# A gate stage as one stream of shifted pieces, and a basic block whose bands run ahead in hand order

## The chip, the cores and the metric

The kernel runs on one core of a Trainium2 chip. The time is that of one execution on the device, in microseconds. "Before" is the median of three runs; the profile is one further execution, with its own time.

## The reference

The input x is fp32, of shape 2 x 128 x 128 x 128 (images, channels, rows, columns). Four layers follow each other:

```python
x = layer0(x)   # 3x3 convolution, 8-token mamba scan per pixel, group norm, SiLU, + x
x = layer1(x)   # density gate, see below
x = layer2(x)   # as layer0, with other weights
x = layer3(x)   # basic block, see below
```

The density gate, with 8x8 windows and four groups of 32 channels:

```python
g = x as (B * 4 groups * 16 * 16 windows, 32 channels, 64 pixels)
sq = sum(g * g, -1);  gram = g @ g.T
K = exp(-0.5 * max(sq[:, :, None] + sq[:, None, :] - 2 * gram, 0))
density = K.mean(-1)                      # B x 128 x 16 x 16
y = w2 @ relu(w1 @ density + b1) + b2     # 128 -> 32 -> 128 channels
attn = sigmoid(y) + 0.5
return x * upsample_bilinear(attn, 8)     # back to 128 x 128, corners aligned
```

The basic block, with convolution weights replaced by their signs:

```python
out = relu(batchnorm(conv3x3(x, sign(w1))))
out = batchnorm(conv3x3(out, sign(w2)))
return relu(out + x)
```

Both batch norms take their statistics over the whole batch and all pixels, so each convolution ends before its normalisation begins.

## The kernel before

Channels lie on the 128 partitions. The program is a chain of stages: `_mamba` (layer 0), `_gates` (layer 1), `_mamba` (layer 2), `_basic_block` (layer 3). A mamba layer leaves its result y, before group norm, in device memory; the stage behind it loads y and the layer's input, and makes `Silu(scale * y + bias) + input`. In `_mamba` the order on all engines is written by hand, under `tc.manual_schedule`. In `_gates` and `_basic_block` the Tile planner chooses the order on each engine; instructions that stand outside a hand order can be placed around it. Within an engine, and on the queues on which SP and ACT issue DMAs, instructions run in their order, and one that waits holds those behind it.

**`_gates`.** Work goes by bands of 8 rows: 16 per image, 32 in all, 512 KB each. `load` (L629) loads y and x, applies Silu on ACT (L636) and adds on POOL (L638), into `x1`, a tile with one 8x8 window after another. `turn` (L646) transposes the band on PE (L652) into `pt`; DVE copies it (`xt`, L654), ACT squares it (`xq`, L656) and squares the untransposed band (`sq`, L659), which DVE reduces (`nsq`, L661 and L662). `density` (L665) sums norms and the Gram matrices of all windows in one PSUM tile `pg` (L671 and L681), adds the second norm on DVE (L689), clips on POOL (L695) and takes Exp on ACT (L696). `total` (L699) reduces to densities. Only when an image's last band is through does `gain` (L702) compute the gate for all of its 256 windows: two small products, Relu, Sigmoid, plus 0.5 (L707 to L720). Then `apply` (L722) runs over the image's 16 bands: PE spreads the gains with interpolation weights `ct` (L738, products with K=32 that take one or two of the image's window-row segments at a time), DVE multiplies with the band (L747), and ACT's queue stores it (L751). Image 0's applications alternate with image 1's densities; image 1's come at the end. PSUM has two wide buffers `pt` (3 banks each) and `pg` (2 banks).

**`_basic_block`.** Again 32 bands of 8 rows. `combine` (L814) forms four sums and differences of rows (a Winograd transform in the row direction): number 0 and 3 on POOL (L818, L821), 1 and 2 on DVE (L819, L820). `conv` (L824) does 12 products of 512 columns for the eight rows (L828; each is recorded in two parts, so 24 a band), in the order 1, 2, 0, 3; ACT copies product 1 out (L836), DVE forms the rows of Y (L839 to L842) and their statistics (L844). `convolve` (L860) combines band k + 1 ahead of the products of band k:

```python
ahead = combine(band(*bands[k + 1])) if k + 1 < len(bands) else None
conv(u, v, *at, stats)
```

In the first convolution `band` is `first` (L870): load of y and residual with a border of one row, Silu (L876), add on POOL (L877), and a store of the sum to x3 on ACT's DMA queue (L878). In the second it is `second` (L887): two rows copied from the band before (L894), the others by Relu from Y (L900). Bands have two buffers, `comb` two, `xs` three. The last loop (L908 to L913) loads x3 into one of the three `xs`, takes `Y * s2 + x3` on DVE, Relu on ACT, and stores on ACT's queue.

Of the kernel before, what the change touches and what calls it, by code (L numbers as in the profile page):

```python
# [31 lines left out]
P = 128  # L32
# [59 lines left out]
def _place(k):  # L92


    q = k // 2
    return k % 2 + 2 * (q // 4), q % 4


def _upsampling(H):

    _, fy = _bilinear(H)
    ix, fx = _bilinear(P)
    wx = np.zeros((P // WIN, P), np.float32)
    wx[ix, np.arange(P)] = 1.0 - fx
    wx[ix + 1, np.arange(P)] += fx
    segs = _segments(H)
    up = np.zeros((4, 2, P // WIN, 4, max(e - a for _, a, e in segs), P), np.float32)
    for k, a, e in segs:
        n, g = _place(k)
        for h in range(a, e):  # L110
            up[g, 0, :, n, h - a] = (1.0 - fy[h]) * wx
            up[g, 1, :, n, h - a] = fy[h] * wx
    return up.reshape(P, 4, -1)
# [488 lines left out]
def _gates(tc, src, w, con, y, stats, wm, b1, up, dst, H):  # L602

    nc = tc.nc
# [3 lines left out]
    nwin = nh * nw  # L608
    segs = _segments(H)
    with tc.tile_pool(name="dg", bufs=2) as dp, tc.tile_pool(name="dg1", bufs=1) as sp, tc.tile_pool(  # L610
        name="ps_t", bufs=2, space=PSUM
    ) as pst, tc.tile_pool(name="ps_g", bufs=1, space=PSUM) as psg:

        def wide():
            return pst.tile([P, 3 * ROWS, P], F32, tag="pt", name="pt")

        class Small:


            def tile(self, shape, dtype, tag=None, name=None):  # L620
                return wide().rearrange("p a b -> p (a b)")[: shape[0], : shape[1]]

        norm = [_norm(nc, sp, Small(), w, con, stats, b) for b in range(B)]
        ct = sp.tile([P, 4, up.shape[2]], F32, tag="ct", name="ct")

        dens = [sp.tile([P, nh, 2, npair], F32, tag=f"dens{b}", name="dens") for b in range(B)]
        held, live, gains = {}, {}, {}

        def load(b, y0):  # L629

            rows = slice(y0 * WIN, (y0 + 1) * WIN)
            g = dp.tile([P, WIN, P], F32, tag="g", name="g", bufs=4)
            nc.sync.dma_start(out=g, in_=y[b][:, rows, :])
            xr = dp.tile([P, WIN, P], F32, tag="xr", name="xr", bufs=4)
            nc.sync.dma_start(out=xr, in_=src[b][:, rows, :])
            nc.scalar.activation(g, g, AF.Silu, bias=norm[b][1], scale=norm[b][0])  # L636
            x = held[b, y0] = dp.tile([P, nw, WIN, WIN], F32, tag="x1", name="x1", bufs=nh + 5)
            nc.gpsimd.tensor_tensor(by_row(x), by_row(xr, False), by_row(g, False), ALU.add)  # L638
# [6 lines left out]

        def turn(b, y0):  # L646

            x = held[b, y0].rearrange("p x r w -> p (x r w)")

            pt = wide()[:, :npair, :]  # L650
            for k in range(npair):
                nc.tensor.transpose(pt[:, k, :], x[:, k * P : (k + 1) * P], con["ident"])  # L652
            xt = dp.tile([P, npair, P], F32, tag="xt", name="xt")
            nc.vector.tensor_copy(xt, pt)  # L654
            xq = dp.tile([P, npair, P], F32, tag="xq", name="xq")
            nc.scalar.activation(xq, pt, AF.Square)  # L656

            sq = dp.tile([P, nw, WIN * WIN], F32, tag="sq", name="sq", bufs=1)
            nc.scalar.activation(sq.rearrange("p x r -> p (x r)"), x, AF.Square)  # L659
            nsq = dp.tile([P, nw], F32, tag="nsq", name="nsq")  # L660
            nc.vector.tensor_reduce(nsq, sq, AX.X, ALU.add)  # L661
            nc.vector.tensor_scalar_mul(nsq, nsq, -0.5)  # L662
            live[b, y0] = xt, xq, nsq

        def density(b, y0):  # L665
            xt, xq, nsq = live.pop((b, y0))

            pg = psg.tile([P, 2, 512], F32, tag="pg", name="pg")
# [19 lines left out]
            kk = dp.tile([P, 2, npair, CG], F32, tag="kk", name="kk", bufs=3)  # L688
# [6 lines left out]
            nc.gpsimd.tensor_scalar_min(kk, kk, 0.0)  # L695
            nc.scalar.activation(kk, kk, AF.Exp)  # L696
            live[b, y0] = kk

        def total(b, y0):  # L699
            nc.vector.tensor_reduce(dens[b][:, y0], live.pop((b, y0)), AX.X, ALU.add)  # L700

        def gain(b):  # L702

            den = sp.tile([P, nh, npair, 2], F32, tag="den", name="den")
            nc.vector.tensor_scalar_mul(den, dens[b].rearrange("p y a k -> p y k a"), 1.0 / CG)
            p1 = wide().rearrange("p a b -> p (a b)")[:CG, :nwin]
            nc.tensor.matmul(p1, lhsT=wm["w1"], rhs=den.rearrange("p y k a -> p (y k a)"), start=True, stop=True)  # L707
            hid = sp.tile([CG, nwin], F32, tag="hid", name="hid")
            nc.scalar.activation(hid, p1, AF.Relu, bias=b1)
            p2 = wide()[:, :4, :]  # L710
            gt = gains[b] = sp.tile([P, 4, P], F32, tag="gain", name="gain")
            for n in range(4):
                at = (n % 2 + n // 2 * WIN) * nw
                m = min(P, nwin - at) // 32 * 32
                if m <= 0:
                    continue
                nc.tensor.matmul(p2[:m, n, :], lhsT=hid[:, at : at + m], rhs=wm["w2"], start=True, stop=False)
                nc.tensor.matmul(p2[:m, n, :], lhsT=wm["one"][:, :m], rhs=wm["b2"], start=False, stop=True)
                nc.scalar.activation(gt[:m, n, :], p2[:m, n, :], AF.Sigmoid)
                nc.vector.tensor_scalar_add(gt[:m, n, :], gt[:m, n, :], 0.5)  # L720

        def apply(b, y0):  # L722

            r0 = y0 * WIN
            pu = wide()
            o = dp.tile([P, WIN, P], F32, tag="g", name="o", bufs=4)
            x = by_row(held.pop((b, y0)))

            cut = [a for k, a, _ in segs if k % 2 == 0 and r0 < a < r0 + WIN]
            at = 0  # L730
            for first, end in zip([r0, *cut], [*cut, r0 + WIN]):
                for r in range(first, end, ROWS):
                    for k, a, e in segs:
                        lo, hi = max(a, r), min(e, r + ROWS, end)
                        if lo < hi:
                            n, g = _place(k)
                            q = slice(g * 32, (g + 1) * 32)
                            nc.tensor.matmul(  # L738
                                pu[:, at + lo - first : at + hi - first, :],
                                lhsT=gains[b][q, n, :],  # L740
                                rhs=ct[q, n, (lo - a) * P : (hi - a) * P],
                                start=True,
                                stop=True,
                                tile_position=(q.start, 0),
                            )
                rows = slice(first - r0, end - r0)
                nc.vector.tensor_tensor(  # L747
                    by_row(o[:, rows, :], False), by_row(pu[:, at : at + end - first, :], False), x[:, rows], ALU.mult
                )
                at += (end - first + ROWS - 1) // ROWS * ROWS  # L750
            nc.scalar.dma_start(out=dst[b][:, r0 : r0 + WIN, :], in_=o)  # L751

        order = [(b, y0) for b in range(B) for y0 in range(nh)]
        N = len(order)
        ready = []
        for n in range(-4, N + 2):
            if ready:
                apply(*ready.pop(0))
            if n % 2 == 0:
                for i in range(n + 4, min(n + 6, N)):  # L760
                    load(*order[i])
            if n == -4:
                nc.sync.dma_start(out=ct, in_=up)
            if 0 <= n < N:
                turn(*order[n])
            if 1 <= n <= N:
                density(*order[n - 1])
            if n >= 2:
                b, y0 = order[n - 2]
                total(b, y0)  # L770
                if y0 == nh - 1:
                    gain(b)
                    ready += [(b, i) for i in range(nh)]
        for at in ready:
            apply(*at)


def _basic_block(tc, src, y, norm, x3, w1, w2, bn, out, B, H):
# [6 lines left out]
    with tc.tile_pool(name="bb", bufs=1) as cp, tc.tile_pool(name="bband", bufs=2) as bp, tc.tile_pool(  # L785
# [28 lines left out]
        def combine(xb):  # L814

            v = combined()
            d = [xb[:, k : k + BAND - 1 : 2, :] for k in range(4)]
            nc.gpsimd.tensor_tensor(v[:, 0], d[0], d[2], ALU.subtract)  # L818
            nc.vector.tensor_tensor(v[:, 1], d[1], d[2], ALU.add)  # L819
            nc.vector.tensor_tensor(v[:, 2], d[2], d[1], ALU.subtract)  # L820
            nc.gpsimd.tensor_tensor(v[:, 3], d[1], d[3], ALU.subtract)  # L821
            return v
# [173 lines left out]
```

## Time and profile before

| | |
|---|---|
| median of 3 runs | 7862.33 us (7861.02 to 7884.91) |
| profiled execution | 7862.75 us, span 7860.9 us |
| mean granted TensorE clock | 0.923 of full speed |
| PE busy | 6537.9 us (83%) |
| DVE busy | 6831.1 us (87%) |
| ACT busy | 4291.8 us (55%) |
| POOL busy | 5521.1 us (70%) |
| gate stage, first load to next layer's first load | 3328 to 3638 us |
| first convolution's products | 6980 to 7390 us |
| second convolution's products | 7400 to 7733 us |
| last loop | 7742 to 7861 us |

Busy shares over the whole span say little here: nearly 6900 us of it are the two mamba layers. The stages are read by windows of time. In a table by windows each engine has its busy time and in brackets the instructions counted; then come the granted TensorE clock as a share of full speed, the mean busy share of the 16 DMA engines, and GB/s. In a list of waits each line names who waited and for what it waited last, then the total in us, the number of times and the longest. In the timeline a line has start, length, engine, line of the kernel, operation, tiles and shapes, and in square brackets the idle time before it with its releaser. PEld is the weight load beside PE; SPq and ACTq are issues of DMAs.

### The profile page before, as it was taken

The page shows a single profiled execution, that of the slowest core. Times are in us where ns is not written, and L with a number is a line of the kernel's source. Part 1 is how long each engine was busy: PE and PEld are TensorE (multiplying, and loading weights), DVE is VectorE, ACT ScalarE, POOL GpSimd, SP SyncE. Part 2 cuts the span into 40 slices and gives each one's busy share as a digit, 9 for nine tenths or more (in the row PEclk, how much of TensorE's full clock was granted, in tenths as well). Part 3 has the DMA queues.
Part 4 walks back from the last instruction along what each step waited for, and adds up shares of the span by engine and source line. Part 5 has one row for each costly group of instructions (what it writes and reads, how often), then busy time and mean ns, then how long its engine had stood idle before and what let it go on. Part 6 is the DMA issues. An engine that isn't in the chain of part 4 may idle for free. (4 is left out here: it accounts for less than half of the span.)

```text
span 7860.9 us, 86792 instructions
## 1 busy us (share of the span) xinstructions
PE 6537.9 (83%) x29412; PEld 2217.4 (28%) x29412; DVE 6831.1 (87%) x6360; ACT 4291.8 (55%) x4835; POOL 5521.1 (70%) x1810
## 2 busy tenths in 40 slices
PE   7888888888888888777888888888888888878893
PEld 2222222222222222253222222222222222223341
DVE  5999999999999999863999999999999999963454
ACT  5656666666666656482665665666656656621112
POOL 5777887777778777652777778787777777843330
PEclk8999999999999999866999999999999999979996
DMA  7999999999999999854999999999999999955204
GB/s 203 246 243 246 253 249 247 253 250 256 249 248 254 245 249 248 225 179 127 244 249 246 250 250 251 252 251 253 252 239 249 250 250 250 250 157 139 69 0 163
DMA packets 573435, 1765.42 MB, mean 225 GB/s; under 512 B 85536, under 2 KB 239680, under 8 KB 458176
## 3 DMA queue, kind: packets, MB, share of 16 engines
q1 hardware_dynamic: 530496, 1709.54, 84.0%
q10 hardware_dynamic: 42496, 50.34, 1.8%
q8 instruction: 234, 3.83, 0.2%
q14 instruction: 209, 1.71, 0.1%
HBM read 1549.82 MB, written 209.72 MB: 224 GB/s over the span
## 5 line engine op out<-in xcount | busy, mean ns | idle before, releaser
L451 POOL TENSOR_TENSOR h<-ur,bcr 128x2048 f32<-128x2048 f32 x896 | 4060.4, 4539 | 1193.2 <-DMA bcr<-sb 1006.0
L478 DVE TENSOR_TENSOR set<-set,h 128x1024 f32<-128x1024 f32 x1792 | 2193.0, 1224 | 301.6 <-ACT set L469 216.2
L479 DVE TENSOR_TENSOR r<-set,bcr 128x1024 f32<-128x1024 f32 x1792 | 2194.1, 1224 | 61.4
L469 ACT ACTIVATE set<-set 128x1024 f32<-128x1024 f32 x1792 | 1745.6, 1006 | 868.7 <-PE set L460 854.2
L483 DVE TENSOR_TENSOR h<-set,h 128x1024 f32<-128x1024 f32 x1536 | 1864.5, 1214 | 21.3 <-POOL h L451 21.2
L460 PE MATMUL set<-dt,rep 32*128 32x512 f32 x7168 | 1400.2, 674 | 96.8 <-DVE h L483 89.9
L498 PE MATMUL ys<-r,ct 128*32 128x512 f32 x7168 | 1166.1, 632 | 36.4 <-DVE r L479 36.0
L328 PE MATMUL one<-band,conv 128*128 128x512 f32 x2304 | 1085.5, 607 | 24.6 <-DMA band<-in_x_dram 12.2
L828 PE MATMUL m<-comb,u 128*128 128x512 f32 x1536 | 689.1, 610 | 88.5 <-DVE Y L842 53.2
L406 PE MATMUL one<-xc,keep 128*64 128x512 f32 x1024 | 324.6, 717 | 471.4 <-ACT xc L363 361.5
L460 PEld LDWEIGHTS set<-dt,rep 32*128 32x128 f32 x7168 | 405.2, 193 | 992.7 <-issue 466.2
L328 PEld LDWEIGHTS one<-band,conv 128*128 128x128 f32 x2304 | 408.2, 190 | 674.4 <-issue 599.2
L489 PE MATMUL ys<-t,ct 128*128 128x512 f32 x512 | 326.4, 724 | 252.4 <-DVE v L511 250.9
L357 ACT ACTIVATE xc<-one,keep 128x512 f32<-128x512 f32 x256 | 176.1, 688 | 519.5 <-PE one L355 514.7
L498 PEld LDWEIGHTS ys<-r,ct 128*32 128x32 f32 x7168 | 181.2, 111 | 928.5 <-issue 760.7
L828 PEld LDWEIGHTS m<-comb,u 128*128 128x128 f32 x1536 | 296.6, 195 | 480.3 <-issue 457.3
L426 PE MATMUL one<-prod,ct 128*128 128x512 f32 x512 | 290.3, 650 | 123.1 <-POOL prod L418 88.8
L380 POOL TENSOR_TENSOR u<-dt,xc 128x1024 f32<-128x1024 f32 x128 | 302.8, 2366 | 70.7 <-ACT dt L374 70.6
L355 PE MATMUL one<-y,w_in 128*128 128x512 f32 x512 | 343.5, 759 | 5.8 <-ACT xc L357 3.1
L469 ACT ACT_TABLE_LOAD x252 | 323.3, 1283 | 4.6
L370 PE MATMUL one<-xc,w_dt 128*128 128x512 f32 x512 | 313.5, 696 | 4.1 <-ACT bc L413 4.1
L427 ACT COPY t<-one 128x512 f32<-128x512 f32 x256 | 150.2, 587 | 301.4 <-PE one L426 301.4
(136 smaller groups left out, 5894.0 us busy)
## 6 DMA issues: line engine op xcount, KB each, us to landing
ur<-su SPq DMA_DIRECT2D x896, 896.0 KB, 11.5
bcr<-sb SPq DMA_DIRECT2D x896, 448.0 KB, 11.6
ur<-su SPq DMA_DIRECT2D x896, 128.0 KB, 11.1
su<-u SPq DMA_DIRECT2D x1024, 64.0 KB, 3.5
sb<-bc SPq DMA_DIRECT2D x256, 224.0 KB, 2.8
bcr<-sb SPq DMA_DIRECT2D x896, 64.0 KB, 10.9
y<-o SPq DMA_DIRECT2D x128, 256.0 KB, 9.2
band<-in_x_dram SPq DMA_DIRECT2D x28, 640.0 KB, 10.9
```

The costliest lines, as they stand in the source:

```text
L328: nc.tensor.matmul(py.rearrange("p (r w) -> p r w", r=ROWS), lhsT=w["conv"][:, tap, :], rhs=xb[:, r + kh : r + kh + ROWS, kw : kw + P], st ...
L355: nc.tensor.matmul(p, lhsT=w[("in", "z")[i]][:, g, :], rhs=s["y"], start=True, stop=True)
L406: nc.tensor.matmul(p[g * NQ * DS : (g + 1) * NQ * DS, :], lhsT=w[("xb", "xcm")[i]], rhs=s["xc"][:, g, :], start=True, stop=True,)
L451: nc.gpsimd.tensor_tensor(b, s["ur", t], s["bc", t][:, 0].unsqueeze(1).to_broadcast([P, NJ, NS]), ALU.mult)
L460: nc.tensor.matmul(a[j // 2][:, j % 2, :], lhsT=w["rep"][r, q, :], rhs=s["dt"][r, g, :], start=True, stop=True, tile_position=(r.start, 0),)
L469: nc.scalar.activation(x, x, AF.Exp)
L478: nc.vector.tensor_tensor(pt, pt, s["h", t - 1][:, js, :], ALU.mult)
L479: nc.vector.tensor_tensor(s["r", t][:, js, :], pt, s["bc", t - 1][:, 1].unsqueeze(1).to_broadcast([P, 2, NS]), ALU.mult)
L483: nc.vector.tensor_tensor(s["h", t][:, js, :], pt, s["h", t][:, js, :], ALU.add)
L489: nc.tensor.matmul(s["ys", g], lhsT=con["ident"], rhs=s["t1"][:, g, :], start=True, stop=False)
L498: nc.tensor.matmul(s["ys", g][a : a + NQ * DJ, :], lhsT=red[:, q, :], rhs=r[:, j, :], start=False, stop=(q == NQ - 1), tile_position=(0, a),)
L828: nc.tensor.matmul(m[:, i], lhsT=u[:, i, kw, :], rhs=v[:, i, :, kw : kw + P], start=(kw == 0), stop=(kw == 2),)
```

## The change

The gate stage becomes one stream over all 32 bands. Every band passes through 14 pieces (load and residual ahead of them), each with a lag in steps, in an order written by hand for all five engines:

```diff
+        stages = (
+            (3, density),
+            (6, hide_relu),
+            (8, gate_exp),
+            (1, norms),
+            (2, distance),
+            (0, turn),
+            (4, total),
+            (9, gain),
+            (10, apply),
+            (10, keep),
+            (1, gram),
+            (7, gate),
+            (5, hide),
+            (9, spread),
+        )
+        E = mybir.EngineType
+        with tc.manual_schedule(engines={E.PE, E.Activation, E.DVE, E.Pool, E.SP}):
+            for n in range(-6, N + 11):
+                if n % 2 == 0:
+                    for m in range(max(n + 4, 0), min(n + 6, N)):
+                        load(*order[m])
+                    for m in range(max(n + 2, 0), min(n + 4, N)):
+                        residual(*order[m])
+                for lag, stage in stages:
+                    if stage is gram and 0 <= n + 6 < N and order[n + 6][1] == 0:
+                        b = order[n + 6][0]
+                        norm[b] = _norm(nc, sp, psg, w, con, stats, b)
+                    if 0 <= n - lag < N:
+                        stage(*order[n - lag])
```

The gate is computed for four window rows around a band as soon as these are known, instead of for a whole image; the sigmoid is formed from Exp, an add and a reciprocal; each band is spread by two products with K=64, whose weights are laid out per band (4.19 MB for all bands instead of 2.36 MB):

```diff
+        def gate(b, y0):
+            s = live[b, y0]
+            p = s["pz"] = psg.tile([P, P], F32, tag="two", name="pz")
+            h = hidden[b][:, y0 : y0 + 4, :].rearrange("p y x -> p (y x)")
+            for a in range(0, P, P // 2):
+                nc.tensor.matmul(p[a : a + P // 2, :], lhsT=h, rhs=wm["w2"], start=True, stop=False)
+                nc.tensor.matmul(p[a : a + P // 2, :], lhsT=wm["one"], rhs=wm["b2"], start=False, stop=True)
+
+        def gate_exp(b, y0):
+            s = live[b, y0]
+            s["e"] = dp.tile([P, P], F32, tag="e", name="e")
+            nc.scalar.activation(s["e"], s.pop("pz"), AF.Exp, scale=-1.0)
+
+        def gain(b, y0):
+            e = live[b, y0]["e"]
+            nc.vector.tensor_scalar_add(e, e, 1.0)
+            nc.vector.reciprocal(e, e)
+            nc.vector.tensor_scalar_add(e, e, 0.5)
+
+        def spread(b, y0):
+            s = live[b, y0]
+            pu = s["pu"] = pst.tile([P, 2 * ROWS, P], F32, tag="pt", name="pu")
+            for n in range(2):
+                q = slice(n * P // 2, (n + 1) * P // 2)
+                nc.tensor.matmul(
+                    pu[:, n * ROWS : (n + 1) * ROWS, :].rearrange("p r w -> p (r w)"),
+                    lhsT=s["e"][q, :],
+                    rhs=weights[q, y0, :],
+                    start=True,
+                    stop=True,
+                )
+
+        def keep(b, y0):
+            nc.sync.dma_start(out=dst[b][:, y0 * WIN : (y0 + 1) * WIN, :], in_=live.pop((b, y0))["o"])
```

`hide` and `hide_relu` are the product with w1 and the Relu for one band's 16 windows. `turn`, `norms`, `gram`, `distance`, `density`, `total` and `apply` are the old operations cut into pieces; `apply` is now one multiplication of 128x1024. The two `pt` buffers shrink to two banks each and are shared by the transposes and the spreading. The band stores go to SP's queue. Image 1's normalisation moves from the head of the stage into step 10.

In the basic block three band rooms take the place of two buffers, all four combines go to POOL, and both convolutions get a hand order with loads three bands, making two bands and combining one band ahead:

```diff
-            nc.gpsimd.tensor_tensor(v[:, 0], d[0], d[2], ALU.subtract)
-            nc.vector.tensor_tensor(v[:, 1], d[1], d[2], ALU.add)
-            nc.vector.tensor_tensor(v[:, 2], d[2], d[1], ALU.subtract)
-            nc.gpsimd.tensor_tensor(v[:, 3], d[1], d[3], ALU.subtract)
+            for i, (m, n, op) in enumerate(((0, 2, ALU.subtract), (1, 2, ALU.add), (2, 1, ALU.subtract), (1, 3, ALU.subtract))):
+                nc.gpsimd.tensor_tensor(v[:, i], d[m], d[n], op)
...
+            v = {}
+            E = mybir.EngineType
+            with tc.manual_schedule(engines={E.PE, E.Activation, E.DVE, E.Pool, E.SP}):
+                for k in range(-3, len(bands)):
+                    for ahead, f in ((3, load), (2, make)):
+                        if 0 <= k + ahead < len(bands):
+                            f(k + ahead)
+                    if 0 <= k + 1 < len(bands):
+                        v[k + 1] = combine(k + 1)
+                    if k >= 0:
+                        conv(u, v.pop(k), *bands[k], stats)
...
+        def residual(k):
+            b, r0 = bands[k]
+            xb, lo, hi = span(k)
+            x = xb[:, lo:hi, 1 : P + 1]
             nc.scalar.activation(x, x, AF.Silu, bias=norm[b][1], scale=norm[b][0])
-            nc.gpsimd.tensor_tensor(x, x, xs, ALU.add)
-            nc.scalar.dma_start(out=x3[b][:, r0 : r0 + BAND, :], in_=xb[:, 1 : BAND + 1, 1 : P + 1])
+            nc.gpsimd.tensor_tensor(x, x, rests.pop(k), ALU.add)
+            nc.sync.dma_start(out=x3[b][:, r0 : r0 + BAND, :], in_=xb[:, 1 : BAND + 1, 1 : P + 1])
```

The x3 store moves from ACT's queue to SP's. The rooms' side columns are cleared once instead of for every band. In the last loop the loads of x3 alternate between two `xs` buffers and the two `comb` buffers:

```diff
-        for b, r0 in bands:
-            xr = rest()[:, :BAND, :]
+        for k, (b, r0) in enumerate(bands):
+            if k % 2 == 0:
+                xr = rest()[:, :BAND, :]
             else:
...
+                xr = combined().rearrange("p a b c -> p (a b c)")[:, : BAND * P].rearrange("p (r w) -> p r w", r=BAND)
             nc.sync.dma_start(out=xr, in_=x3[b][:, r0 : r0 + BAND, :])
```

## The prediction

> **What bounds the kernel now.** I read the busy time by stretches first, to see which stages the change touches and what each is limited by.
>
> ```profile
> core 0: us, PE busy (x) PEld busy (x) DVE busy (x) ACT busy (x) POOL busy (x), PEclk, DMA share, GB/s
> 3328.00:3447.00 119.00, 65.50 (x2592) 53.20 (x2592) 67.13 (x84) 110.28 (x105) 72.75 (x37) 0.70 0.64 222
> 3447.00:3460.00 13.00, 11.26 (x162) 6.17 (x162) 7.33 (x14) 9.75 (x13) 2.97 (x2) 0.50 0.00 1
> 3460.00:3570.00 110.00, 96.12 (x2216) 61.26 (x2216) 74.25 (x91) 59.12 (x61) 46.76 (x25) 0.70 0.41 146
> 3570.00:3584.00 14.00, 11.40 (x28) 6.63 (x29) 3.19 (x8) 2.85 (x6) 0.00 (x0) 0.50 0.19 75
> 3584.00:3638.00 54.00, 47.11 (x80) 22.68 (x78) 19.19 (x22) 0.00 (x0) 0.00 (x0) 0.50 0.37 146
> 6980.00:7390.00 410.00, 356.27 (x768) 150.19 (x767) 159.25 (x249) 61.99 (x62) 164.13 (x129) 0.95 0.49 133
> 7400.00:7733.00 333.00, 332.50 (x768) 146.04 (x768) 186.14 (x249) 55.98 (x63) 112.63 (x127) 0.99 0.00 0
> 7742.00:7861.00 119.00, 0.00 (x0) 0.00 (x0) 39.96 (x33) 36.61 (x32) 0.00 (x0) 0.50 0.79 269
> ```
>
> The gate stage (3328 to 3638) takes 310 us in five pieces: image 0's densities (ACT 110 of 119 us busy), its gain, image 1's densities beside image 0's application, the second gain, and an application alone (all PE, at half clock). The two convolutions do the same 768 recorded matmul parts; the second keeps PE busy throughout, the first takes 77 us longer. The last loop uses neither PE nor POOL, and moves 269 GB/s at a DMA share of 0.79. The two mamba layers, ahead of and behind the gate stage, are not touched.
>
> Next, the waits of 6980 to 7390, and one band there in the timeline:
>
> ```profile
> ACT band L876 <- DMA band<-y: 237.8, 30, 16.8
> DVE Y L839 <- ACT m L836: 233.2, 30, 9.0
> POOL band L877 <- ACT band L876: 199.3, 29, 7.5
> ACT m L836 <- POOL band L877: 82.3, 25, 3.8
> PE m L828 <- DVE Y L842: 53.2, 25, 3.9
> ```
>
> ```profile
> 7184.49 0.37 SPq L198 DMA_DIRECT2D band<-y  x1
> ...
> 7189.86 1.45 ACT L876 ACTIVATE band<-band,aff_t,aff_s 128x1280 f32<-128x1280 f32 x1 [8.75 <-DMA band<-y]
> 7191.39 2.68 POOL L877 TENSOR_TENSOR band<-band,xs 128x1280 f32<-128x1280 f32 x1 [6.92 <-ACT band L876]
> ...
> 7194.10 0.42 ACTq L878 DMA_DIRECT2D x<-band  x1
> 7194.62 0.59 ACT L836 COPY m<-m 128x512 f32<-128x512 f32 x1 [3.31 <-PE m L828]
> 7195.24 0.69 DVE L839 TENSOR_TENSOR Y<-m,m 128x512 f32<-128x512 f32 x1 [8.60 <-ACT m L836]
> ```
>
> It is a ring. A band loads (5.4 us), gets Silu (1.45) and the residual (2.7); ACT issues the x3 store, which waits for POOL, and only then evacuates the previous band's product (0.59). DVE's four Y operations (2.4), queued behind that copy, release PE, and the third combine behind them frees a band buffer for the next load. The terms make about 14 us; band loads are issued 12 to 14 us apart, against 10.3 us of products. PE waits for Y although Y is short.
>
> **Conv 1: -77.** The change gives bands three rooms, loads them three ahead, makes them two ahead and combines one ahead; the x3 store leaves ACT's queue for SP's. Evacuation now waits only for PE. PE becomes the bound, as in the second convolution: 410 - 333 = 77 us (24 parts at 0.43 us each, 10.3 us a band). What must stay below 10.3: ACT, 1.45 + 0.59; DVE, 4 x 0.60 + 1.28; POOL, which now does all four combines.
>
> Here the Trainium skill speaks against the change ("GPSIMD Engine Reference", 4.1 Engine selection): an elementwise add belongs on VectorE, GpSimd being about twice as slow with two inputs. The row agrees in size: 1.29 us for a 128x520 combine on POOL alone (L818), 0.69 on DVE (L819). But the rule prices the operation, not the path: POOL needs 4 x 1.29 + 2.69 = 7.85 us a band, 9.7 with the 1.75 us that such a combine takes when it collides with DVE; both are under 10.3. By the rule alone I would add 2 x 0.6 x 64 = 77 us and cancel the gain; by the row I add nothing, as long as the cover of 10.3 us holds.
>
> The order on POOL is copy of the product after PE ends, Silu, add, combine: ready for its first product (combines 0 and 1) 0.6 + 1.45 + 2.7 + 2.6 = 7.4 us after the previous band's end, 2.9 us to spare. SP has 0.37 + 0.32 + 0.42 us of issues a band; the x3 store waits there for POOL's add, with the next loads behind it. They were asked for three bands ahead, and have about 5 us to spare after a 5.6 us landing.
>
> **Starts: +3.** Before the first product POOL does combines 0 and 1 in series (2.6 us) where DVE did number 1 alone (0.7). After the normalisation there is a 0.4 us row copy too: +2.3 us. In conv 1 the weights' preparation hides most of it: +0.7. If the planner places that preparation badly around the hand order, up to 8 more; at best 0.
>
> **Last loop: -18.** Its bands pass through three buffers; now two of xs and two of comb. A round lasts about 11 us (load 4.3, DVE 1.28, ACT 1.15, store 3.6 to 6): 11/3 = 3.7 us a band, as measured (119/32). Four buffers give 11/4 = 2.75, if the queues allow. 269 GB/s at a share of 0.79 means 340 GB/s at 1.0, and a band moves 1.05 MB: 3.1 us. I take 3.2 for 28 bands, with four preloaded: about 101 us, -18. Bounds: -32 at 2.75, -8 at 3.6.
>
> **Gate stage: -41.** Each band now walks through one stream of 32 + 10 steps; the separate gain pauses (27 us) and the lone application (54 us) go. I price one full step by engine.
>
> DVE, start to start: norms 1.40, distance 0.62, copy of the transpose 1.14, total 0.60, apply 1.15, and the gain (three operations of 128x128 in sequence). The adds are 0.23 each (L720). RECIPROCAL appears only as 128x1, at 160 ns against 154 for TENSOR_SCALAR. Low price: 0.23, like the add. High: the Trainium skill ("VectorE: DVE Perf Modes", the walkthrough's hardware budget) says an iterative divide with a repeat count of 8; at 1.05 ns an element (slope from 128x512 to 128x1024) an estimate of 1.2 us. No row excludes either; the 6 ns excess favours the upper, so I take 1.0. Sum 6.4. Small SBUF-only operations are also held up by POOL: L662 has a median of 174 ns but reaches 1473, L720 reaches 2058; mean excesses of 0.2 and 0.35 us, for four operations about 0.8. DVE: 7.2 us (5.6 with a cheap reciprocal and no collision).
>
> ACT: 1.19 Silu, 1.30 table loads (two per two bands), 0.6 Exp, 2.0 Squares, 0.5 for Relu and gate Exp: 5.6. The sigmoid's own table load goes, since Exp serves both. POOL: 2.36 + 1.49 = 3.85. SP: four loads and two stores every second step, 2.2 us of issue in 14; 1.5 MB a step at the 222 GB/s seen here would take 7.1 us, but 408 GB/s were reached at 3335 to 3345, so 3.9.
>
> PE: transposes 1.09 us at full clock (1.97 at half), square sums 0.66 (1.11), Gram 1.5 (1.6), gate 0.43 (0.85), hide 0.1 (0.2), spreading 0.86 (1.7): 4.6 (7.5). The last takes K=64 products in two row halves to run side by side. This line supports that:
>
> ```profile
> 3298.30 1.53 PE L460 MATMUL set<-dt,rep 32*128 32x512 f32 x8
> ```
>
> Eight 512-column parts in 1.53 us, where one after another they would need 3.4. Without overlap, PE is 5.5 to 9.2.
>
> Which clock? The skill's rule ("TensorE: Matmul & The Clock Gate", Part 1) is full rate after one busy window of about 3.4 us. The trace contradicts it here: 3584 to 3638 has PE busy 47 of 54 us and a clock of 0.50 throughout, with K=32 products. By the rule PE needs 4.6 us a step and never decides; by that row 7.5. Mixed with transposes and Gram products the rows show 0.70, so I take about 0.75, 6.0 us, under DVE's 7.2.
>
> Sum: the first Silu 3334 becomes 3336, as the table of upsampling weights ahead of the loads grows from 2.36 to 4.19 MB (the old one landed in 8.8 us). Step 0 takes 8 us (four Silus); steps 1 to 9 follow ACT, 9 x 6.0 = 54; image 1's normalisation in mid-stream 4; 22 steps x 7.2 = 158; ten draining steps 32 (DVE's total, gain and apply, about 3.2 each); the store's landing 4.5. End near 3597 instead of 3638: -41. With the cheap DVE step ACT and DVE, both at 5.6, make about 5.9 with a few waits: 22 x 1.3 = 29 more, -70.
>
> **Total.** The profiled execution took 7862.75 us (span 7860.9, 1.9 around it), 0.4 above the shown median. 7862.75 - 41 - 77 + 3 - 18 = 7729.75, so 7730.
>
> **Rivals.**
> - *PE at half clock becomes the stream's bound* (20%): 7.5 us plus waits for the single Gram buffer, 9.0 a step: 22 x 1.8 = 40 us eat the gate's gain. 7730 + 41 = 7771. For it: the 0.50 row; against: full-array transposes and Gram in every step.
> - *Everything fits better* (12%): 5.9 a step, last loop at 2.75: -70 - 77 + 3 - 32 gives 7687.
> - *The distances are not there in effect* (4%): loads stay queued behind the x3 store on SP, and conv 1 keeps its 12.8 us a band: 7730 + 77 = 7807. Against: three bands' lead.
> - *Slower* (4%): in the stream PE and DVE take turns, since transposes need the copy, Gram the distance's buffer and spreading the gain, all in hand order. The chain: norms 1.4, distance 0.6, square sums and Gram 2.7, gate 0.85, spreading 1.7, transposes 2.0, copy 1.2, total 0.6, gain 1.5, apply 1.15: 13.7 us. With steps 1 to 31 at that and the drain at 6, the stage ends at 3336 + 8 + 4 + 425 + 60 + 4.5 = 3837, 199 later than before: 7862.75 + 199 - 92 = 7970. It decides from 11.1 us a step over steps 1 to 31 (6.8 forecast, plus 133/31). Against: nearly every piece is a step behind what it needs.
>
> **How the numbers follow.** The forecast has 60%, 7705 to 7755 by its own terms. A range of 7688 to 7782 takes in the half-clock case, and leaves out the last two and part of the good one. A measurement can tell 0.3%, 24 us, from no change. Faster 0.95, same 0.01, slower 0.04.
>
> **What would show it.** Conv 1 at 330 to 335 us with PE busy and no "PE m waits for DVE Y"; POOL 8 to 10 us a band; last loop near 101 us; gate stage 250 to 285 us, DVE first in busy time in its full steps, RECIPROCAL 128x128 near 1 us. Wrong if POOL's combines take 2 us and more, if ACT again waits for POOL, or if the stream's full step is over 8.5 us.

## The result, and the profile after

After takes 7759.15 us (median of four runs, 7755.61 to 7763.59), before 7867.67 (four runs on the same chip, 7861.02 to 7884.91): a ratio of 0.9859, 95% interval 0.9841 to 0.9877. The forecast was 7730 within 7688 to 7782; the narrower 7705 to 7755, which the prediction held for 60% likely, was missed by 4 us. The profiled execution of after took 7763.59 us, with a span of 7761.8: 99.1 less than before's 7860.9, where the prediction summed to 133.

First the windows of after, with the same columns as before: the stream, its drain, conv 1, conv 2, the last loop.

```profile
3405.00:3576.00 171.00, 126.74 (x3656) 84.79 (x3655) 146.80 (x207) 112.84 (x151) 78.78 (x42) 0.83 0.46 167
3576.00:3616.00 40.00, 29.56 (x252) 12.87 (x252) 30.39 (x48) 5.89 (x18) 3.36 (x5) 0.57 0.36 145
6970.00:7303.00 333.00, 331.87 (x768) 145.87 (x768) 116.73 (x186) 57.70 (x62) 225.84 (x161) 0.99 0.52 165
7313.00:7647.00 334.00, 331.92 (x768) 145.88 (x768) 116.75 (x186) 52.58 (x62) 159.10 (x160) 0.99 0.01 2
7656.00:7762.00 106.00, 0.00 (x0) 0.00 (x0) 40.29 (x33) 36.62 (x32) 0.00 (x0) 0.50 0.84 297
```

Conv 1 now has PE busy throughout, as conv 2. The last loop moves 297 GB/s where it moved 269. In the stream DVE has the most busy time, 147 of 171 us, and nothing else is near full. That row misleads, as the experiments show.

The waits of conv 1 (6970 to 7303) in after:

```profile
DVE Y L873 <- ACT m L870: 210.5, 31, 15.5
POOL band L924 <- ACT band L923: 89.4, 29, 5.2
PE m L862 <- POOL comb L855: 26.0, 1, 26.0
```

PE's only large wait is the one at the start (26.0, once). "PE m waits for DVE Y", 53.2 us before, is gone.

By stage, the two profiled executions give (conv 1 from its first to the start of its last product; the end from the last product of conv 2 to the end of the span):

| us | before | after | fall |
|---|---|---|---|
| mamba 1 (end) | 3321.0 | 3322.4 | -1.4 |
| gate stage | 317.5 | 293.2 | 24.3 |
| mamba 2 | 3312.4 | 3324.7 | -12.3 |
| mamba 2 to conv 1 | 28.8 | 30.2 | -1.4 |
| conv 1 | 409.1 | 331.3 | 77.8 |
| conv 1 to conv 2 | 11.2 | 13.3 | -2.1 |
| conv 2 | 331.9 | 331.3 | 0.6 |
| to the end | 129.0 | 115.4 | 13.6 |

Mamba 2, whose code is unchanged, is 12 us longer. Over the 14 profiled executions of this study mamba 1 ended between 3309.5 and 3339.1 us and mamba 2 took 3298.0 to 3328.6, with old and new gate stages alike (standard deviations 10 and 9 us). That is scatter of the two untouched stages: one kernel alone, `e2_gates_only`, ranged over 42 us in 20 runs. It is large enough to hide 10 us in a total, so the experiments below are read by stage.

### The profile page after: what moved, and what is told of

The parts are those of the page before. It is cut to its first block, busy times and chain, and to the rows that moved or that the text cites. A ratio compares the mean times of both kernels' runs of the same rounds, so it can differ in the third digit from the quotient of the medians.

```text
span 7761.8 us, 87240 instructions
## 1 busy us (share of the span) xinstructions
PE 6470.4 (83%) x29648; PEld 2196.5 (28%) x29648; DVE 6759.3 (87%) x6304; ACT 4272.3 (55%) x4873; POOL 5628.0 (73%) x1879
## 4 chain that ended last, share of the span: by engine, by line
DVE 35%; DMA 31%; PE 19%; issue 6%; POOL 4%; ACT 4%; SPq 2%; POOLq 0%; DVEq 0%; ACTq 0%
DMA bcr<-sb 24%; DVE set L471 12%; DVE h L476 10%; DVE r L472 10%; PE m L862 9%; DMA ur<-su 3%; POOL h L444 3%; PE one L348 2%; PE set L453 2%; ACT set L462 1%; PE one L399 1%; PE ys L491 1%; DVE v L504 1%; PE ys L482 1%; DMA band<-in_x_dram 1%
## 5 line engine op out<-in xcount | busy, mean ns | idle before, releaser
L862 PE MATMUL m<-comb,u 128*128 128x512 f32 x1536 | 663.8, 595 | 38.7 <-POOL comb L855 38.7
L873 DVE TENSOR_TENSOR Y<-m,m 128x512 f32<-128x512 f32 x64 | 43.9, 687 | 436.2 <-ACT m L870 436.2
L855 POOL TENSOR_TENSOR comb<-band 128x520 f32<-128x520 f32 x256 | 298.2, 1198 | 162.4 <-PE m L862 160.4
L870 ACT COPY m<-m 128x512 f32<-128x512 f32 x64 | 37.5, 586 | 556.8 <-issue 474.7
## 6 DMA issues: line engine op xcount, KB each, us to landing
bcr<-sb SPq DMA_DIRECT2D x896, 448.0 KB, 11.8
ur<-su SPq DMA_DIRECT2D x896, 128.0 KB, 11.2
```

Source lines behind the costliest of these rows:

```text
L862: nc.tensor.matmul(m[:, i], lhsT=u[:, i, kw, :], rhs=v[:, i, :, kw : kw + P], start=(kw == 0), stop=(kw == 2),)
```

## The experiments

**The two halves alone.** `e1_bands_only` is before with the new basic block; `e2_gates_only` is after with the old one.

```diff
# e1_bands_only: before, but
-def _basic_block(...)   # before's
+def _basic_block(...)   # after's
# e2_gates_only: after, but
-def _basic_block(...)   # after's
+def _basic_block(...)   # before's
```

> The basic block of after in the kernel of before; the gate stage is the old one. Theory (the two parts add up, and each gives what its own stretch showed): conv 1 falls from 410 to about 333 us, the last loop from 120 to about 106, the starts cost 3, so 7862 - 88, about 7775 us (7765 to 7785), the gate stage ends where it did (about 3638 us) and mamba 2 takes its 3312 us of before, because its 12 us more in after came with the new gate stage. Rival (the 12 us are the run's own scatter and have nothing to do with the change): mamba 2 lands anywhere from 3310 to 3326 us here, and the total between 7765 and 7790.

> The gate stage of after in the kernel of before; the basic block is the old one. Theory (the parts add up): the gate stage ends about 23 us earlier than before (near 3615 us), conv 1 stays at 410, the last loop at 120; total 7840 us if mamba 2 keeps its 3312 us. If the new gate stage itself makes mamba 2 longer by 12 us (its stores now go out on SP's queue and its weights lie elsewhere), mamba 2 takes about 3325 us and the total is about 7852. Rival (scatter): mamba 2 is as often short as long.

Measured: `e1_bands_only` took 7778.37 us, ratio 0.9885 (0.9843 to 0.9926), and `e2_gates_only` 7843.65 us, ratio 0.9968 (0.9955 to 0.9981), against a before of 7873.89 on that chip. The product of the ratios is 0.9853, after's own 0.9859: within these intervals the halves add up. Conv 1 took 331.3 and 408.4 us, as its code says. Mamba 2 took 3317.5 with the old gates and 3310.7 with the new, so the 12 us did not come with the gate stage. The gate stage took 328.5 and 290.7.

Over all profiles with code left as it is, the old gate stage took 317.5, 328.5, 316.7 and 314.3 us (mean 319.3), the new one 287.8 to 293.5 in seven (mean 291.3). The change is worth **28.0** there, more than the first pair showed. The end falls from a mean of 131.7 (four) to 116.4 (nine): **15.3**.

**What conv 1 owes its 78 us to.** Three parts undone one at a time:

```diff
# e3_no_distance: load, Silu and add one band ahead, in the step of the combines
-for ahead, f in ((3, load), (2, make)):
+for ahead, f in ((1, load), (1, make)):
# e4_dve_combines: combines 1 and 2 on DVE again
-nc.gpsimd.tensor_tensor(v[:, i], d[m], d[n], op)
+(nc.vector if i in (1, 2) else nc.gpsimd).tensor_tensor(v[:, i], d[m], d[n], op)
# e6_store_act: the x3 store on ACT's queue again
-nc.sync.dma_start(out=x3[b]..., in_=xb...)
+nc.scalar.dma_start(out=x3[b]..., in_=xb...)
```

> Loading and making moved from 3 and 2 bands ahead to 1 band ahead, all in one step with the combining; the hand order, four combines on POOL and the store on SP stay. Theory (the distances carry the 77 us: without them Silu, add and four combines follow a load that has only just been issued): one chain per band of about 5 us of load, 1.5 of Silu, 1.4 of add and 4 x 1.2 of combining is 12.5 to 13 us, longer than PE's 10.3, so conv 1 goes back to 390 to 420 us and PE waits for POOL's comb in every band. Rival (it was DVE's queue: the two combines on DVE stood behind the add and ahead of Y, and with them gone PE keeps its bank whatever the distance): conv 1 stays at 333 to 345 us.

> Combines 1 and 2 back on DVE, the distances kept. Theory (only the distances matter; DVE has 3.65 us of work in a 10.3 us band and two combines of about 0.7 to 1.5 us fit): conv 1 stays within 333 to 336 us, DVE's busy time rises by 32 x 1.4 to 3 us = 45 to 95, POOL's falls by 32 x 2.4 = 77, total as after (7755 to 7770). Rival (the move of the combines to POOL carries the gain, because a DVE combine that waits for POOL's add holds up Y): conv 1 goes to 360 us or more, with PE waiting for DVE Y.

> After with the x3 store issued on ACT's queue again, as before; distances, hand order and the four combines on POOL stay. Theory A (the ring of before was closed by POOL's memset ahead of every band load, and the store on ACT was only a part of it that a band made two ahead can carry): conv 1 from first to last product stays within 331 to 336 us. Theory B, that of the prediction (the copy of m stood behind the store's wait for POOL's add; that must go): the copy waits for POOL's band again, 2 to 3 us a band, and conv 1 takes 350 to 410 us.

Measured, conv 1: 337.9, 331.4 and 331.0 us (totals of single runs 7754.66, 7769.0 and 7765.64). The distances, which I had held for the reason, are worth 6.6 us; the place of the combines and of the store, each undone alone, nothing. In `e3_no_distance` the ring left over is add, store on SP, load behind it, Silu, add. Over the 32 bands SP issues the stores 9.9 to 11.8 us apart, 10.7 at the median: the ring runs just over PE's 10.3, and the 6.6 us are this excess. In `e4_dve_combines` the combines on DVE took a median of 1.78 us and those on POOL 1.75, against 0.69 and 1.29 alone, and still did no harm: DVE was busy 199 of 333 us. The combines and the store were not undone together.

Next a ring put in, and the old code freed of what I thought closed it:

```diff
# e7_memset_no_distance: e3 with before's memset of the borders ahead of each load, on POOL
 def border(k):
     xb, lo, hi = span(k)
+    nc.gpsimd.memset(xb[:, :, 0 : P + 2 : P + 1], 0.0)
# e9_old_two_rooms: before, bands in two fixed tiles, borders cleared once
-xb = _load_band(nc, bp, y[b], r0, BAND, H)
+xb = room[r0 // BAND % 2]          # plus the edge rows and the load, as there
# e10_old_three_rooms: e9 with three
+xb = room[(b * H + r0) // BAND % 3]
```

> The kernel with all of a band one step ahead (337.9 us for conv 1), with one instruction more per band: the memset of the two border columns on POOL ahead of each band load, which every band had before. Theory A (POOL's order memset, load, Silu, add, combines, next memset is a ring with no overlap): 0.12 + about 5.3 from memset to Silu + 1.35 + 2.44 + 4.65 of combines = 13.9 us a band, conv 1 430 to 460 us, PE waiting for POOL's comb in nearly every band. Theory B (the ring was closed by the store on ACT's queue or by the two combines on DVE, and a memset of 0.1 us costs nothing): conv 1 stays at 335 to 345 us.

> The kernel of before with one thing changed: its bands lie in two fixed rooms whose border columns are cleared once at the start, so that no memset stands in POOL's queue ahead of a band load (edge rows at the image's ends are still cleared). The planner's order, two combines on DVE, the store on ACT and the old gate stage stay. Theory A (the memset closed the ring): conv 1 falls from 409 to 335 to 360 us. Theory B (the store on ACT and the combines on DVE close it): conv 1 stays at 395 to 410 us.

> The kernel of before with three fixed rooms for its bands in place of two, their borders cleared once; the planner's order, two combines on DVE, the store on ACT and the old gate stage stay. Theory A (with two rooms the next band load waits for a combine that stands in POOL's queue behind the add of the band before: add 2.68, combines 2.55, load 6.1, Silu 1.46 make 12.8 us in series, which is what a band of conv 1 took with two rooms; the third room lets the load start a band earlier): conv 1 falls from 408.5 to 331 to 345 us, from one more room alone. Theory B (the store on ACT's queue, ahead of the copy of m, or the combines on DVE hold it): 390 us or more, with the copy still waiting for POOL's band.

Conv 1 took 438.5, 408.5 and 403.8 us. The first is Theory A's: one memset of 0.12 us, standing in POOL's queue behind one band's combines and ahead of the next band's load, costs 100 us, for the load then waits for the combines too and not for the add alone:

```profile
7139.27 2.35 POOL L856 TENSOR_TENSOR comb<-band 128x520 f32<-128x520 f32 x2
...
7141.57 0.12 POOL L844 MEMSET band<- 128x20 f32 x1
...
7141.71 0.36 SPq L916 DMA_DIRECT2D band<-y  x1
```

The waits of that kernel, 6975 to 7300:

```profile
ACT band L924 <- DMA band<-y: 204.0, 23, 16.8
PE m L863 <- POOL comb L856: 50.9, 23, 4.4
```

The other two refute what I expected of before: without the memset the old code is as slow as with it (409.1), and a third room gains 5 us. The timeline of `e10_old_three_rooms` shows why:

```profile
7139.85 2.68 POOL L886 TENSOR_TENSOR band<-band,xs 128x1280 f32<-128x1280 f32 x1 [8.46 <-ACT band L885]
7142.48 1.29 POOL L818 TENSOR_TENSOR comb<-band 128x520 f32<-128x520 f32 x1
...
7143.73 1.29 POOL L821 TENSOR_TENSOR comb<-band 128x520 f32<-128x520 f32 x1
...
7145.05 0.37 SPq L881 DMA_DIRECT2D band<-y  x1
...
7150.89 1.46 ACT L885 ACTIVATE band<-band,aff_t,aff_s 128x1280 f32<-128x1280 f32 x1 [7.22 <-DMA band<-y]
```

The load goes out at 7145.05, as the last combine on POOL ends (7145.02). Counted up to there, it is the 19th band load, after the 18th add and the 16th pair of POOL combines. The 19th band takes the room of the 16th, and the 16th's combines stand in POOL's queue behind the 18th's add. In before, with two rooms, the lag is one band: the 13th load went out after the 12th add and the 11th band's last combine. The planner let the combines fall behind by as many bands as there were rooms to spare, so the third room bought almost nothing, and load, Silu, add and combines again followed one another.

That is one band in two. In every other band the combine that frees the room last is number 2 on DVE (L820):

```profile
7155.13 0.42 ACTq L887 DMA_DIRECT2D x<-band  x1
7155.64 0.59 ACT L836 COPY m<-m 128x512 f32<-128x512 f32 x1 [3.30 <-POOL band L886]
...
7158.66 0.69 DVE L820 TENSOR_TENSOR comb<-band 128x520 f32<-128x520 f32 x1
...
7159.41 0.37 SPq L881 DMA_DIRECT2D band<-y  x1
```

It stands behind DVE's four operations on Y, these behind ACT's copy, and the copy behind the x3 store, which waits for POOL's add (it ends at 7155.10). Here the load follows the add by 4.3 us, in the other bands by 2.5; in before by 4.5 and 2.7, in the same alternation. So the prediction's ring is there, in half of the bands.

Both rings run through the places that the planner gave the combines in the queues. If so, the written order is the part that counts. `e11_planner_order` keeps everything of after's basic block but that:

```diff
-with tc.manual_schedule(engines={E.PE, E.Activation, E.DVE, E.Pool, E.SP}):
+if True:
```

> After with the two convolutions of the basic block in the planner's order in place of the written one; three rooms, distances as written in the loop, four combines on POOL, the store on SP and the gate stage of after stay. In the built program POOL's queue then has each band's four combines behind the add of the band two further on. Theory A (the combines that free a room stand in POOL's queue behind an add that itself waits for the load into that room's neighbour, so that load, Silu, add and combines run in series): 5.5 + 1.46 + 2.68 + 4.8 = 14.4 us a band, conv 1 420 to 465 us from first to last product, slower than the 409 of before since two more combines are in the ring. Theory B (the written order is not needed once bands have three rooms, no memset and no store on ACT): 331 to 345 us.

Conv 1: 403.9 us, below the 420 to 465 of Theory A, but of its kind (I had the load 1.3 us too long). Its timeline:

```profile
7154.87 0.36 SPq L915 DMA_DIRECT2D band<-y  x1
7159.04 1.45 ACT L923 ACTIVATE band<-band,aff_t,aff_s 128x1280 f32<-128x1280 f32 x1 [11.08 <-DMA band<-y]
...
7160.57 2.68 POOL L924 TENSOR_TENSOR band<-band,xs 128x1280 f32<-128x1280 f32 x1 [5.73 <-ACT band L923]
...
7163.21 4.65 POOL L855 TENSOR_TENSOR comb<-band 128x520 f32<-128x520 f32 x4
...
7167.88 0.36 SPq L915 DMA_DIRECT2D band<-y  x1
```

4.2 + 1.5 + 2.7 + 4.6 = 13.0 us from load to load, the next one 0.02 us after the combines. The ring is not quite that of before: the store has left ACT's queue and no combine is on DVE, but four combines on POOL stand behind the add. With the rest of the change in place, the written order is worth 72.6 of the 77.8 us: it puts each band's combines straight behind the add of the following band and not of the one after that, so that a room is free before its load is due. What it would be worth alone, in before's code with two rooms, was not run.

**The gate stage: is DVE its bound?** Without the RECIPROCAL:

```diff
# g2_no_recip
 nc.vector.tensor_scalar_add(e, e, 1.0)
-nc.vector.reciprocal(e, e)
 nc.vector.tensor_scalar_add(e, e, 0.5)
```

> After without the RECIPROCAL of the gates (the gates are then 1.5 + exp(-z) in place of 0.5 + sigmoid(z), and so is everything behind them); the two additions stay. Theory A, that of the prediction (DVE bounds the full step): 20 full steps lose 0.95 us each, the gate stage (last o copy of mamba 1 to first band load of mamba 2) falls from 288 to 294 us by 17 to 21 us, DVE's busy time by 32 x 0.95 = 30. Rival (PE at its reduced clock, with its own gaps of issue, sets the step, and DVE's share only looks full): the stage falls by less than 6 us.

The stage took 299.0 us: not shorter, 6 longer than after's 293.2. DVE's busy time in 3424 to 3573 fell from 134.7 to 127.2 us. DVE's busy time is not the bound. What is, shows in two steps of after's timeline, from one pair of Silus to the next:

```profile
3428.68 2.37 ACT L635 ACTIVATE g<-g,aff_t,aff_s 128x1024 f32<-128x1024 f32 x2
...
3430.01 4.70 POOL L637 TENSOR_TENSOR x<-xr,g 128x1024 f32<-128x1024 f32 x2 [8.07 <-ACT g L635]
...
3433.49 1.30 DVE L737 TENSOR_SCALAR e<-e 128x128 f32<-128x128 f32 x1
...
3434.94 2.08 PE L745 MATMUL pu<-up,e 64*128 64x512 f32 x4
...
3436.95 1.76 PE L646 MATMUL pt<-ct,x 128*128 128x128 f32 x8
...
3438.74 1.23 DVE L648 COPY xt<-pt 128x1024 f32<-128x1024 f32 x1 [0.90 <-PE pt L646]
...
3440.07 1.02 ACT L650 ACTIVATE xq<-pt 128x1024 f32<-128x1024 f32 x1 [2.73 <-DVE xt L648]
...
3440.99 1.05 ACT L652 ACTIVATE sq<-x 128x1024 f32<-128x1024 f32 x1
...
3442.05 1.28 ACT L635 ACT_TABLE_LOAD   x1
...
3443.35 2.37 ACT L635 ACTIVATE g<-g,aff_t,aff_s 128x1024 f32<-128x1024 f32 x2
```

It is a ring through the queues of four engines: Silu, POOL's two adds (4.7); DVE's add of 0.5, which takes 0.23 alone and here runs 1.30, until POOL is through; spreading; behind it on PE the transposes; the copy; the two squares; a table load; and only then, in ACT's order, the next Silus. That is 14.7 us for two steps; the median of the pairs is 14.9. No engine is full, and what DVE does while it is held costs nothing. In `g2_no_recip` the two remaining additions stood in that gap instead:

```profile
3460.57 4.67 POOL L637 TENSOR_TENSOR x<-xr,g 128x1024 f32<-128x1024 f32 x2 [6.45 <-ACT g L635]
...
3461.57 1.44 DVE L735 TENSOR_SCALAR e<-e 128x128 f32<-128x128 f32 x1
...
3463.04 2.28 DVE L736 TENSOR_SCALAR e<-e 128x128 f32<-128x128 f32 x1
```

The second ends at 3465.3, the adds at 3465.2. That the stage even grew has another reason: in this build the spreading also waits for DVE's multiplication `o`, 14.4 us in eight times between 3424 and 3573, which it does not in after. The pairs took 16.0 us at the median. In the pair shown spreading began at 3466.6 and could have begun about 1.1 us earlier; by that estimate a pair would be as long as after's, and not shorter. Why the wait came in was not found.

The Trainium skill has this behaviour ("SBUF — State Buffer", Who interferes with whom): VectorE's `tensor_scalar` on SBUF operands can enter a mode that needs a port pair shared with GpSimd, and the later of the two then waits for the whole of the other's instruction. These rows agree: each of the two ends 0.08 us after the end of one of POOL's adds. The RECIPROCAL, on SBUF too, was never held in after (3424 to 3573; count, then shortest, median and longest in ns):

```profile
L736 DVE RECIPROCAL e<-e x20: 952/952/953, 3426.1 to 3569.0; 128x128 f32<-128x128 f32 x20
L737 DVE TENSOR_SCALAR e<-e x20: 226/227/1300, 3427.1 to 3569.9; 128x128 f32<-128x128 f32 x20
```

So the small operations were to leave DVE:

```diff
# v1_tanh: sigmoid(z) + 0.5 = (tanh(z / 2) + 2) / 2, the last half in the weights
-nc.scalar.activation(s["e"], s.pop("pz"), AF.Exp, scale=-1.0)
+nc.scalar.activation(s["e"], s.pop("pz"), AF.Tanh, scale=0.5)
-nc.vector.tensor_scalar_add(e, e, 1.0)
-nc.vector.reciprocal(e, e)
-nc.vector.tensor_scalar_add(e, e, 0.5)
+nc.gpsimd.tensor_scalar_add(e, e, 2.0)
# and: Square with scale 0.5 ** 0.5, a subtraction in distance, no product with -0.5
```

> After with the gates made in another way: sigmoid(z) + 0.5 = (tanh(z/2) + 2) / 2, Tanh on ACT, one addition of 2.0 on POOL, the half in the upsampling weights; the norms' factor -0.5 goes into Square's scale and a subtraction. DVE loses the two additions, the RECIPROCAL and the small product. Without the RECIPROCAL alone the stage did not fall (299 against 288 to 294 us): its two additions then stood for 3.7 us while POOL's two adds of 4.67 us ran. Theory A (DVE is held by POOL's adds through these small operations, whatever else it has to do in that time): without them a pair of steps falls from 14.3 us by 1.5 to 3.5, the stage from about 292 to 250 to 275 us. Theory B (PE with its reduced clock and its waits for ACT's e and xq sets the step): the stage falls by less than 6 us.

A miss: 299.3 us, with DVE down to 85.9 of the 149 us from 134.7. A third of DVE's busy time gone from the stream, and nothing gained: I had put the new addition into the ring itself:

```profile
3453.69 4.68 POOL L637 TENSOR_TENSOR x<-xr,g 128x1024 f32<-128x1024 f32 x2 [7.55 <-ACT g L635]
...
3458.34 1.49 POOL L695 TENSOR_SCALAR kk<-kk 128x512 f32<-128x512 f32 x1
...
3459.79 0.53 POOL L734 TENSOR_SCALAR e<-e 128x128 f32<-128x128 f32 x1
...
3460.38 2.08 PE L742 MATMUL pu<-up,e 64*128 64x512 f32 x4 [1.99 <-POOL e L734]
```

It stood behind the adds and the minimum, and PE waited for it (20.1 us in nine times between 3424 and 3573): 16.6 us a pair at the median.

**A version from these readings.** `v2_all` takes everything out from behind POOL's adds and mends the last loop:

```diff
 nc.scalar.activation(s["e"], s.pop("pz"), AF.Tanh, scale=0.5)
+nc.scalar.activation(e, e, AF.Relu, bias=two)      # tanh + 2, on ACT
-nc.gpsimd.tensor_scalar_min(kk, kk, 0.0)
# both norms at n == -6; b2 as a 33rd row of the gate's product
# last loop: the three band rooms too, xr = two xs, two comb, three rooms in turn
```

> A version made from the readings so far. Gate stage: tanh form as in v1_tanh, but the addition of 2.0 on ACT (Relu with a bias) directly behind Tanh, and no minimum with 0 on POOL, so that POOL keeps only its two adds of a pair and nothing of the stream stands behind them; the second layer's bias as a 33rd row of the product (four products of K=32 less a step); both images' normalisation at the head. Last loop: seven tiles in place of four for the transfers. Basic block as in after. Theory A (a pair of steps is a ring through in-order queues: Silu, POOL's adds, what stands behind them on DVE or POOL, spread, transposes, copy, squares, table load, Silu; 16.0 to 16.4 us without the RECIPROCAL and in v1_tanh): with nothing behind the adds ACT is the longest, 2.56 of table loads + 2.4 of Silu + 2 x 3.5 = 12 us a pair, so the stage falls from 292 to 240 to 265 us. Rival (PE at 0.5 to 0.8 of its clock and its gaps of issue are the bound): a pair stays at 14 us or more and the stage at 275 us or more, less about 8 for the normalisation. Last loop: with about 353 GB/s at full DMA share the floor is 3.1 us a band, from last product to the end 115 to 118 falls to 106 to 112 us. Total by A: 7700 to 7730 us.

7692.97 us (7682.76 to 7704.51), ratio to before 0.9794 (0.9777 to 0.9811), where after has 0.9859; the two were timed on different chips. By stage it gains on the mean of after 22.7 us in the gate stage (268.6, a little over what I expected) and 28.9 at the end (87.5, well under it): 51.6, and the two ratios differ by 51 us of 7860. The median pair of steps took 13.5 us from Silu to Silu, for 14.9 in after; I had expected 12. Not all of the gate stage's gain is the ring: beside after's own profile (24.7 us longer) the 20 full steps are 13.0 us shorter, and moving the normalisation saves 10.2 in steps 10 and 11 and costs 2.7 at the head. The parts were not run singly. The last loop, after's waits first (7656 to 7762), then `v2_all`'s window:

```profile
DVE comb L950 <- DMA comb<-x: 38.4, 14, 5.5
DVE xs L950 <- DMA xs<-x: 22.5, 14, 5.2
```

```profile
7620.00:7699.00 79.00, 0.00 (x0) 0.00 (x0) 40.83 (x35) 36.40 (x32) 0.00 (x0) 0.50 0.94 379
```

With four tiles DVE waits 61 of 106 us for landings; with seven nearly the same bytes move at 379 GB/s, in 79.

## Why the prediction was right or wrong

- **Conv 1, -77: right in size** (-77.8), and PE is the bound as said. The ring that it read, through store, copy, Y and the third combine, is there in every second band, the one shown at 7184.49 among them; in the others the load waits for POOL's combines, which it did not name. What undoes the ring it had wrong: not "the x3 store leaves ACT's queue for SP's", since with the written order the store does no harm on ACT (`e6_store_act`, 331.0), and without that order its move leaves 403.9 (`e11_planner_order`). The written order, worth 72.6, was in the change, but no term of the sum rests on it. The rival "The distances are not there in effect", 7807, priced something worth 6.6 us at 77.
- **POOL's cover: right.** I set 7.85 us a band; POOL was busy 225.84 / 32 = 7.1, below the 8 to 10 named as a sign. The rule that an add belongs on VectorE changed nothing in either direction.
- **Starts, +3: right.** +2.1 ahead of conv 2; ahead of conv 1 means of 29.2 and 29.7 us.
- **Last loop, -18: a little mis-sized, -15.3.** "269 GB/s at a share of 0.79 means 340 GB/s at 1.0" was no floor: `v2_all` moved 379 GB/s at 0.94, and the prediction's own 408 GB/s in the gate stage spoke against it. Four tiles still left the loop waiting on round trips.
- **Gate stage, -41: mis-sized, -28.0.** After's own profile ends the stage at 3615.6, 18.6 later than the 3597 forecast. The first Silu came on time (3336.4). The copies of steps 0 to 9 are 6.3 us apart for 6.0 forecast, with step 0 two early: +0.6 together. Image 1's normalisation in mid-stream made steps 10 and 11 take 25.4 us against 18.4: +7.0. The 20 steps behind took 7.45 for 7.2: +5.1. From the last copy to the next layer's first load it is 42.4 against 36.5: +5.9. The drain runs at clock 0.57, one spreading taking 2.08 us and a step 3.7, where I had put DVE's 3.2.
- **The step of the working that failed is that DVE's 7.2 us bound the full step.** They came near the 7.45 measured by luck. RECIPROCAL took 0.95 (1.0 taken), DVE was first in busy time as foretold, and none of it was the bound: that busy time includes the stops behind POOL. The rival in which PE and DVE take turns had the right kind of mechanism, a chain through in-order queues, but ran it through a single step, at 13.7 us; the one measured spans two, at 14.7.
- **PE's clock: near.** 0.83 in the stream, 0.75 taken.
- **Not in the sum:** +12 in mamba 2, which is scatter. By stage means the change is worth 28.0 + 77.8 - 2.6 + 15.3 = 118.5 us; the medians differ by 108.5.

The normalisation's stop, in after:

```profile
3413.32 1.01 DVE L579 BATCH_NORM_AGGREGATE mv<-stats 128x2 f32<-128x192 f32 x1
...
3414.48 0.56 PE L582 MATMUL pm<-mv,ct 128*128 128x1 f32 x2 [5.44 <-DVE mv L579]
...
3415.86 0.59 PE L590 MATMUL pv<-dev,ct 128*128 128x1 f32 x2 [0.83 <-DVE dev L588]
```

A product of one column stood in PE's queue for a DVE result, and PE lost 5.4 us.

## What to carry to other kernels

When a stage is slow and no engine is full, follow one item round until the chain comes back to its engine, through every queue on the way: what an operation stands behind counts more than what it costs (a memset of 0.12 us cost 100, a RECIPROCAL of 0.95 nothing). More buffers help only if the order on each engine frees them in time, so look at the built order before buying rooms. The highest busy time proves nothing until taking work away shortens the stage.

## What the hardware showed that I had not expected

- Small additions on DVE were held by POOL's adds: 0.23 us became up to 2.29. Of the additions that took over 0.4 us, 17 of 18 in after and all 18 in `g2_no_recip` ended 0.08 to 0.09 us after one of POOL's adds ended. Two-input combines on both engines stretched each other, from 0.69 to 1.78 us on DVE and from 1.29 to 1.75 on POOL (medians of `e4_dve_combines`).
- At a DMA share of 0.79, 0.84 and 0.94 the last loop moved 269, 297 and 379 GB/s. The share is not proportional to what moves.
- A mamba stage of 3.3 ms differs by 30 us between profiled executions, with unchanged code.
